# Summing layer 0's softmax denominators from probabilities that DMAs have folded from 128 keys to 64

## The chip, the cores and the metric

The kernel runs on one core of a Trainium2 chip. A core has a matrix engine (TensorE, PE in the profile, with its weight loads shown as PEld), a vector engine (VectorE, DVE), a scalar engine (ScalarE, ACT), GpSimd (POOL), a queue that mostly issues transfers (SyncE, SP) and 16 DMA engines that all queues share. Each engine works through its own instructions in order. The metric is the time of one execution on the device in microseconds (us). Three timed executions of the kernel before took 994.68, 995.34 and 997.74 us; the median, 995.34 us, is what the prediction is held against.

## The reference, cut to what matters

Two cross-attention layers follow each other over the same 128 context tokens. There are 2 batches of 2048 query tokens, width 512 and 16 heads. Only layer 0 is touched, and of it only the sum in the softmax:

```python
qh = (q @ Wq + bq)                                 # 16 heads of 64
attn = einsum('bqhd,bkhd->hbqk', qh, kh) * mask    # masked scores are 0, not -inf
attn = attn - max(attn)                            # one maximum over the whole tensor
attn = exp(attn) * mask
attn = attn / (sum(attn, axis=-1) + 1e-15)         # sum over the 128 keys
out  = einsum('hbqk,bkhd->bqhd', attn, vh) @ Wo + bo
x    = layernorm(out + residual) * gamma + beta
```

Layer 1 repeats the pattern with 16 heads of 32, an ordinary softmax and its own output projection and layer norm.

## The kernel before, in words

The 4096 query tokens are cut into 8 blocks `t` of 512. Layer 0's attention handles a block in 4 groups `g` of 4 heads, so there are 32 steps (t, g). They go in the list `order`: blocks are taken two at a time, and for each group of heads the two blocks come one after the other. Two neighbouring entries of `order` (the same heads, two blocks) form a pair; the loop over `i` handles the 16 pairs. Scores and probabilities are held with the 128 keys on the partitions and the 512 queries along the row. The denominator is therefore a sum over partitions, and TensorE does it with a block of ones as weights.

Everything is issued in program order (`manual_schedule`), so the text of the loop is the order on every engine. Iteration `i` is built like this (from i = 1 on):

- `queries_pair` makes the queries of pair `i` with seven products in Strassen's manner (1, 6, 7, 2, 5, 4, 3 in this order; each is two matmuls, listed as four, because the profile shows every fp32 matmul as two instructions). The results stand in PSUM tiles of two rings of two buffers each, `mm_tile` and `av_tile`. VectorE adds them up (`add`, lines 358 and 360). Between the products, `exponentials0` is called for the two steps of pair i-1.
- `exponentials0` (lines 420 to 434) needs the largest score of the step. VectorE reduces a row of maxima (line 427), scales it (428), ScalarE takes the exponential of two halves (431) and GpSimd multiplies each half with the mask (432).
- `scores0` for the first step of pair `i` (the matmuls of line 394), VectorE multiplies by the mask and finds the partial maxima (406), SP stores them to DRAM (415, tensor `top`) and loads all of them back onto every partition (418, tile `every`). SP waits at line 418 until the store of line 415 has landed.
- `attend0` for the first step of pair i-1: four matmuls with `ones` sum the keys (442, tile `den`), ScalarE copies the sums (444), eight matmuls make the unnormalised outputs `psu` (450), ScalarE copies them (454), and SP stores 8 KB of sums (455) and 512 KB of outputs (458).
- `scores0` for the second step of pair `i`, then `attend0` for the second step of pair i-1.

In this order a round trip ties one iteration to the next: the second step's maxima of iteration i-1 go to DRAM and back (415, 418) and end at line 427 in the middle of iteration i's products. VectorE's adds of products 5, 4 and 3 stand behind line 427 in VectorE's queue. Below, "top1" and "every1" are the store and the load for the second step, "top0" and "every0" those for the first.

A few things differ at the ends. The iterations of the first two blocks (i = 0 to 3) also make the keys. Masks of later blocks are loaded from GpSimd's queue (line 233) and blocks of `xT` from SP's (226). After the loop the last steps are finished, the sums come back from DRAM as reciprocals, and GpSimd multiplies the outputs with them (line 182) ahead of layer 0's projection (625).

## Time and profile before

The profiled execution took 995.52 us on the device; the span from its first to its last instruction is 993.4 us. It stands 0.18 us from the median of the three timed ones.

| engine | busy us | share of the span | instructions |
|---|---|---|---|
| PE | 968.4 | 97% | 4628 |
| DVE | 657.6 | 66% | 1060 |
| POOL | 482.8 | 49% | 403 |
| ACT | 382.2 | 38% | 625 |
| DMA queue of SP | 125.03 MB | 36.9% of 16 engines | 49536 packets |
| DMA queue of POOL | 2.10 MB | 0.7% of 16 engines | 1152 packets |

The groups that the change touches, over the whole run:

| line | engine and operation | count | busy us | mean ns of one |
|---|---|---|---|---|
| 442 | PE, sums with ones, 128 rows by 32 columns | 256 | 34.1 | 605 |
| 450 | PE, outputs psu, 128 by 32 | 512 | 62.6 | 598 |
| 394 | PE, scores, 64 by 128 | 256 | 63.9 | 616 |
| 432 | POOL, mask multiply | 64 | 150.1 | 2367 |
| 444 | ACT, copy of the sums | 32 | 18.8 | 589 |
| 233 | POOL, issue of a mask load, 256 KB | 8 | 4.7 | 583 |

How to read it: several small matmuls run side by side in the array, so the sum of busy time is less than count times mean. The loop of layer 0 takes the first 377 us; the rest is layer 0's projection and all of layer 1. An engine that is busy 97% may still wait here and there, so where a stage is bound is read from the chain of waits and from the timeline of each engine, not from the share. Times in the timelines are microseconds from the start of the span.

### The profile page before, as it was taken

To read this page: it belongs to the slowest core of one execution; us is meant where nothing else is said; L and a number is where in the kernel's file an instruction comes from. 1 tells how busy PE (TensorE), PEld (TensorE's weight loads), DVE (VectorE), ACT (ScalarE), POOL (GpSimd) and SP (SyncE) were. 2 spreads that over 40 slices of the span, in tenths; PEclk is the share of its full clock that TensorE was granted. 3 is DMA by queue.
4 is the path that set the end of the run, shared out by engine and by line. 5 is a ranking of instruction groups with operands and counts; after the bars stand their busy time and mean duration, and the time that the engine had idled before them with its cause. 6 is when DMAs were issued, how large, how long until landed. Compare 5 with 4: busy or idle time off the path is not lost.

```text
span 993.4 us, 12731 instructions
## 1 busy us (share of the span) xinstructions
PE 968.4 (97%) x4628; PEld 450.2 (45%) x4628; DVE 657.6 (66%) x1060; ACT 382.2 (38%) x625; POOL 482.8 (49%) x403
## 2 busy tenths in 40 slices
PE   8999999999999999999999999999999999999896
PEld 4444333333333334474544645545545545446432
DVE  2544645564465543148569879779789699698766
ACT  1133334334433344034544334444344344344251
POOL 1043544543454545695453934926736637445142
PEclk9999999999999999999999999999999999999998
DMA  9314254224223344633632532622724624304211
GB/s 341 135 49 142 56 167 154 54 76 151 69 59 98 123 139 131 197 119 136 257 123 86 222 121 85 258 85 92 274 71 141 243 84 167 124 1 175 82 43 42
DMA packets 51326, 128.46 MB, mean 129 GB/s; under 512 B 9441, under 2 KB 13281, under 8 KB 47681
## 3 DMA queue, kind: packets, MB, share of 16 engines
q1 hardware_dynamic: 49536, 125.03, 36.9%
q0 software_dynamic: 1152, 2.10, 0.7%
q8 instruction: 36, 0.59, 0.3%
q10 hardware_dynamic: 576, 0.53, 0.2%
q14 instruction: 26, 0.21, 0.1%
HBM read 101.46 MB, written 26.18 MB: 128 GB/s over the span
## 4 chain that ended last, share of the span: by engine, by line
PE 72%; DVE 12%; DMA 9%; issue 2%; POOL 2%; ACT 1%; SPq 1%; POOLq 0%; ACTq 0%; DVEq 0%
PE pso L625 18%; PE ps L346 17%; PE st L394 6%; PE pso L970 6%; PE psu L450 5%; DMA r<-rows 5%; PE psq L776 3%; PE den L442 3%; PE mx L827 3%; DVE sums L857 2%; PE s L900 2%; PE u L948 2%; DVE bn L607 2%; PE psq L814 1%; PE psq L327 1%
## 5 line engine op out<-in xcount | busy, mean ns | idle before, releaser
L432 POOL TENSOR_TENSOR sm<-sm,mask 128x1024 f32<-128x1024 f32 x64 | 150.1, 2367 | 214.0 <-ACT sm L431 214.0
L625 PE MATMUL pso<-wo,uT 128*128 128x512 f32 x512 | 229.3, 599 | 1.1 <-POOL uT L182 1.1
L625 PEld LDWEIGHTS pso<-wo,uT 128*128 128x128 f32 x512 | 94.5, 190 | 118.1 <-issue 108.0
L612 POOL TENSOR_TENSOR rstd<-rstd,mhalf 128x1 f32<-128x1 f32 x64 | 35.1, 549 | 222.0 <-DVE shift L616 221.9
L970 PE MATMUL pso<-wq,ctx 128*128 128x512 f32 x256 | 115.1, 600 | 0.0
L406 DVE CUSTOM_DVE_ANT_1 sm<-st,mask 128x1024 f32<-128x1024 f32 x64 | 75.8, 1221 | 45.2 <-issue 18.5
L431 ACT ACTIVATE sm<-sm,ncs 128x1024 f32<-128x1024 f32 x64 | 69.9, 1140 | 73.8 <-DVE ncs L428 73.6
L843 ACT ACTIVATE e<-mx,less 128x128 f32<-128x128 f32 x224 | 61.0, 383 | 83.3 <-DVE less L840 83.3
L924 ACT ACTIVATE p<-p 128x2048 f32<-128x2048 f32 x28 | 53.5, 1911 | 101.2 <-DVE p L919 70.4
L358 DVE TENSOR_TENSOR q<-ps,q 128x512 f32<-128x512 f32 x75 | 51.5, 689 | 55.1 <-PE ps L346 31.0
L919 DVE TENSOR_TENSOR p<-s,p 128x1024 f32<-128x1024 f32 x56 | 65.9, 1218 | 31.4 <-PE s L900 29.7
L346 PE MATMUL ps<-xt,wq 128*128 128x512 f32 x180 | 83.4, 599 | 0.0
L182 POOL TENSOR_TENSOR uT<-uT,r 128x1024 f32<-128x1024 f32 x32 | 75.2, 2358 | 6.6 <-PE psv L536 4.3
L970 PEld LDWEIGHTS pso<-wq,ctx 128*128 128x128 f32 x256 | 46.7, 190 | 57.6 <-issue 50.7
L857 DVE TENSOR_REDUCE sums<-e 128x16 f32<-128x2048 f32 x28 | 63.8, 2278 | 1.1 <-ACT e L851 1.1
L394 PE MATMUL st<-q,k 64*128 64x512 f32 x256 | 63.9, 616 | 0.2 <-DVE q L358 0.2
L450 PE MATMUL psu<-sm,v 128*32 128x512 f32 x512 | 62.6, 598 | 0.0
L346 PE MATMUL ps<-t,s 128*128 128x512 f32 x120 | 56.4, 592 | 0.0
L346 PEld LDWEIGHTS ps<-xt,wq 128*128 128x128 f32 x180 | 33.2, 190 | 46.5 <-issue 44.5
L444 ACT COPY dens<-den 128x512 f32<-128x512 f32 x32 | 18.8, 589 | 86.6 <-PE den L442 86.6
L640 ACT ACTIVATE z<-z,shift,rstd 128x512 f32<-128x512 f32 x32 | 26.0, 813 | 67.7 <-POOL shift L617 67.7
L642 POOL TENSOR_TENSOR y<-z,g 128x512 f32<-128x512 f32 x32 | 40.6, 1269 | 23.1 <-ACT z L640 23.1
(148 smaller groups left out, 1463.3 us busy)
## 6 DMA issues: line engine op xcount, KB each, us to landing
p<-rows SPq DMA_DIRECT2D x28, 1024.0 KB
u<-u SPq DMA_DIRECT2D x32, 512.0 KB
uT<-u SPq DMA_DIRECT2D x32, 512.0 KB
xt<-in_xT_dram SPq DMA_DIRECT2D x16, 512.0 KB
z<-in_x_dram SPq DMA_DIRECT2D x32, 256.0 KB
r<-r SPq DMA_DIRECT2D x32, 256.0 KB
out_dram<-y SPq DMA_DIRECT2D x32, 256.0 KB
r<-rows SPq DMA_DIRECT2D x28, 256.0 KB
```

What stands on the lines that cost most here:

```text
L182: nc.gpsimd.tensor_tensor(u, u, r.unsqueeze(1).to_broadcast([P, 2, TB]), ALU.mult)
L346: nc.tensor.matmul(ps, w[:, c, :], x[c] if isinstance(x, tuple) else x[:, c, :], start=(c == 0), stop=(c == 1),)
L394: nc.tensor.matmul(st[n][:, j, :], k0[rows, 2 * g + n, b * K : (b + 1) * K], q[rows, :], start=True, stop=True,)
L406: nc.vector.tensor_tensor_reduce(out=sm, in0=st[n], in1=masks[t].unsqueeze(1).to_broadcast([P, 2, TB]), scale=1.0, scalar=-3.4028234e38, o ...
L431: nc.scalar.activation(s, s, AF.Exp, bias=ncs[:, i + n : i + n + 1])
L432: nc.gpsimd.tensor_tensor(s, s, masks[t].unsqueeze(1).to_broadcast([P, 2, TB]), ALU.mult)
L450: nc.tensor.matmul(ps[32 * j : 32 * (j + 1), :], v0[:, b, d : d + 32], p[j], start=True, stop=True,)
L625: nc.tensor.matmul(ps, uTs[t, n // 2][:, n % 2, i * P : (i + 1) * P], wo0s[n // 2][:, n % 2, :], start=(n == 0), stop=(n == NE - 1),)
L843: nc.scalar.activation(e[:, r, i, :], ps[1][:, r - 2, i, :], AF.Exp, bias=less[:, r - 2, i : i + 1], scale=scaling,)
L857: nc.vector.tensor_reduce(to.rearrange("p r i o -> p r (i o)"), open_x.pop((t, g)), AX.X, ALU.add)
L919: nc.vector.tensor_tensor(p1[:, at], ps[n], p1[:, at], ALU.subtract)
L970: nc.tensor.matmul(ps, ctxs[t][g][:, i * P : (i + 1) * P], wo1s[:, g, :], start=(g == 0), stop=(g == NG - 1),)
```

## The change

For the first 14 of the 16 pairs the denominators are no longer summed in `attend0`. After the two steps of pair i-1 are masked, `fold(i-1)` issues four DMAs from GpSimd's queue. Two plain copies (512 KB each) put keys 0 to 63 of the pair's first step on partitions 0 to 63 of a tile `f`, and keys 64 to 127 of its second step on partitions 64 to 127. Two accumulating DMAs (512 KB each) then add the other 64 keys of each step to the same rows. `f` so holds both steps, each with 64 rows in place of 128. One iteration later, after `queries_pair` and before the scores, `sums_of_folded(i-2)` sums that tile with eight matmuls of 64 rows by 32 columns, alternating between the upper and the lower 64 partitions and writing to two PSUM tiles; ScalarE copies both and SP stores both.

To make room and to free the ring `av_tile` for this, three things move: product 3 of `queries_pair` takes its PSUM tile from `mm_tile`; the tiles `den` come from a pool of two buffers in place of four; and the rows `g1s`, `b1s` (layer 1's gamma and beta) are loaded after the first list of layer 1's steps, behind `wo1s`, in place of before the loop. The tile `f` has one buffer.

```diff
-            add(c12, product(3, s4[:, g], b22, av_tile), c12)
+            add(c12, product(3, s4[:, g], b22, mm_tile), c12)
...
+        FOLDED = NB // 2 * NG - 2
...
+            pairs0[t, g] = pair
...
+        def store_sums(t, g, ps):
+            den = a2.tile([P, TB], F32, tag="den", name=f"dens0_{t}_{g}")
+            nc.scalar.copy(den, ps)
+            nc.sync.dma_start(
+                den_rows(den_dram, t, g), den.rearrange("(j n) q -> j n q", n=32)[:, 0, :]
+            )
+        def fold(i):
+            f = w1.tile([P, 4, TB], F32, tag="fold", name=f"fold_{i}")
+            p = [pairs0[step].rearrange("p n j q -> p (n j) q") for step in order[2 * i : 2 * i + 2]]
+            rows = [slice(0, P // 2), slice(P // 2, P)]
+            for n in range(2):
+                nc.gpsimd.dma_start(f[rows[n]], p[n][rows[n]])
+            for n in range(2):
+                nc.gpsimd.dma_start(f[rows[n]], p[n][rows[1 - n]], accum_op=ALU.add)
+            folded[i] = f
+
+        def sums_of_folded(i):
+            f = folded.pop(i)
+            ps = [av_tile(f"den0_{i}_{n}") for n in range(2)]
+            for j in range(4):
+                for n in range(2):
+                    rows = slice(n * P // 2, (n + 1) * P // 2)
+                    nc.tensor.matmul(
+                        ps[n][32 * j : 32 * (j + 1), :], ones[rows, :], f[rows, j, :],
+                        start=True, stop=True,
+                    )
+            for n in range(2):
+                store_sums(*order[2 * i + n], ps[n])
...
         def attend0(t, g):
-            ps = av_tile(f"den0_{t}_{g}")
-            for j in range(4):
-                nc.tensor.matmul(ps[32 * j : 32 * (j + 1), :], ones, p[j], start=True, stop=True)
-            den = a4.tile([P, TB], F32, tag="den", name=f"dens0_{t}_{g}")
-            nc.scalar.copy(den, ps)
+            if order.index((t, g)) // 2 >= FOLDED:
+                ps = av_tile(f"den0_{t}_{g}")
+                for j in range(4):
+                    nc.tensor.matmul(ps[32 * j : 32 * (j + 1), :], ones, p[j], start=True, stop=True)
+                store_sums(t, g, ps)
...
-            nc.sync.dma_start(
-                den_rows(den_dram, t, g), den.rearrange("(j n) q -> j n q", n=32)[:, 0, :]
-            )
...
-        g1s, b1s = row(const, g1, "g1"), row(const, b1, "b1")
...
                 queries_pair(p, g, order[2 * i - 2 : 2 * i])
+                if i > 1:
+                    sums_of_folded(i - 2)
+                if i - 1 < FOLDED:
+                    fold(i - 1)
...
             nc.sync.dma_start(wo1s, chunks(wo1))
+            g1s, b1s = row(one, g1, "g1"), row(one, b1, "b1")
```

## The prediction

> **What bounds the kernel now.** I read the page first, then the chain of waits over the loop of layer 0, and then the timelines of PE, DVE, SP and POOL around one iteration.

> ```profile
> PE 968.4 (97%) x4628; PEld 450.2 (45%) x4628; DVE 657.6 (66%) x1060; ACT 382.2 (38%) x625; POOL 482.8 (49%) x403
> ```

> TensorE is busy 97% of the span. The chain of waits for iteration i = 12 (columns: start, length, what) shows no gap:

> ```profile
> 290.40 12.21 PE ps L346 x28
> 302.62 1.92 PE st L394 x8
> 304.54 1.00 PE den L442 x8
> 305.53 1.77 PE psu L450 x16
> 307.31 1.92 PE st L394 x8
> 309.23 0.99 PE den L442 x8
> 310.22 1.77 PE psu L450 x16
> 312.00 12.21 PE ps L346 x28
> ```

> An iteration is 21.6 us of matmuls back to back: products 12.21, twice scores 1.92, sums 1.00 and outputs 1.77. From i = 4 on, only i = 5 breaks it, for 0.2 us. So work taken off TensorE counts, unless the round trip of the maxima then becomes the longer loop. The next views show how near it is. First PE (products 4 and 3 of the same iteration), then DVE, whose bracket is its idle time before:

> ```profile
> 299.02 1.88 PE L346 MATMUL ps<-t,wq 128*128 128x512 f32 x4
> 300.74 1.88 PE L346 MATMUL ps<-xt,s 128*128 128x512 f32 x4
> ```

> ```profile
> 299.33 0.42 DVE L427 TENSOR_REDUCE whole<-every 128x2 f32<-128x256 f32 x1 [1.07 <-DMA every<-top]
> 299.79 0.17 DVE L428 TENSOR_SCALAR ncs<-whole 128x2 f32<-128x2 f32 x1
> 299.86 0.68 DVE L358 TENSOR_TENSOR q<-ps,q 128x512 f32<-128x512 f32 x1
> 300.46 0.74 DVE L360 SCALAR_TENSOR_TENSOR q<-ps,db,q 128x512 f32<-128x512 f32 x1
> 301.12 0.68 DVE L358 TENSOR_TENSOR q<-ps,q 128x512 f32<-128x512 f32 x1
> ```

> DVE stands idle until every1 lands. The two adds that read product 5 end at 301.20, which is 0.46 us after product 3 has started. Before, that is harmless: product 3 has an `av_tile`. Then SP:

> ```profile
> 289.58 0.32 SPq L415 DMA_DIRECT2D top<-top  x1
> 295.90 0.32 SPq L418 DMA_DIRECT2D every<-top  x1
> ...
> 306.22 0.33 SPq L415 DMA_DIRECT2D top<-top  x1
> 309.49 0.32 SPq L418 DMA_DIRECT2D every<-top  x1
> ...
> 310.45 0.76 SPq L458 DMA_DIRECT2D u<-u  x1
> 311.31 0.38 SPq L415 DMA_DIRECT2D top<-top  x1
> ```

> top0 lands after 3.3 us. top1 is issued right behind the 512 KB store of outputs and lands only after 6.3 us (289.58 to 295.90); every1 takes another 3.4, so T, from the issue of top1 to DVE's reduction, is 9.75 us here. In the twelve iterations i = 4 to 15 T is between 8.56 and 10.9 us, mean 9.88.

> **The change part by part.**

> *Sums on TensorE.* For 14 pairs two passes of 0.995 us go and one pass of eight smaller matmuls comes. No row has eight side by side. The `psu` row has four in 0.885 us (1.77 for two groups), the scores two. If all eight overlap, a pass is about 1.0 us and 14 x 0.99 = 13.9 us go; if only four do, it is 1.9 and 1.3 us go. I take 1.0: line 827 issues 32 matmuls with their weight loads in 1.17 us, 37 ns each, so 16 need 0.6 us to issue and issue does not bind. [...]

> *Product 3 in `mm_tile`.* The ring has two buffers and was used by 1, 6, 5, 4; now product 3 takes product 5's buffer and must wait for both adds that read it, which stand behind line 427 on DVE. This is the wait that the change adds. Behind it on PE stand product 3, the new pass, both scores and outputs; behind those stands top1, which the next line 427 waits for. That closes a loop, and its length replaces the sum over PE if it is longer. From DVE's reduction: 1.87 us to the end of the second add and 0.06 to wake PE; product 3 1.81 (300.74 to 302.55); new pass 1.00; scores 1.92 and outputs 1.77 up to the second scores; from those to top1 4.07 (307.24 to 311.31). That is 12.5 us, and with T = 9.75 the loop is 22.25 us against 21.6 now: **+0.65 us per iteration although PE has 1 us less to do**. Its low end is 21.83 (DVE's scan of the second scores ends 3.65 us after they start, and SP then issues at once), its high end 22.5 (T of 10.0). For the 12 iterations i = 4 to 15: +7.8 us, between +3 and +11.

> *The folding DMAs.* Four issues on POOL at 0.56 us, 2.2 us per iteration. POOL works 9.4 us in 21.6, and is free from 305.96 to 315.75. Per fold 1 MB is copied and 1 MB accumulated. The nearest row is a pair of mask loads, 512 KB, from the same queue:

> ```profile
> 219.26 1.12 POOL L233 DMA_DIRECT2D mask<-in_maskT_dram  x2
> ```
> ```profile
> 219.80 0.32 SPq L415 DMA_DIRECT2D top<-top  x1
> 223.77 0.32 SPq L418 DMA_DIRECT2D every<-top  x1
> ```

> The DMA engines are busy with them from 220.5 to 222.5, 262 GB/s; one lands after 3.7 us (median). By the same rate the two copies move in 4.0 us and land about 6.2 us after the first issue (1.2 to the first byte, 1.0 after the last). The accumulates wait for that, on POOL; behind them there stand the next step's masks, 9.8 us later, so this wait is covered. The accumulates move in 4.0 us, or 8.0 if reading both operands counts twice.

> What they meet is the round trip. POOL's masks of the second step end 6.63 us after line 427 (299.33 to 305.96), and top0 goes out 8.4 us after it, so the copies run beside top0. Beside the mask loads top0 took 3.97 us, and 4.39 at 132.96, against 2.8 to 3.6 otherwise: +1.0 us. SP issues nothing until top0 has landed, so the output store and top1 go out that much later. The accumulates start some 13 us after line 427, as does the 512 KB output store that top1 must follow. Alone it moves from 290 to 292.7. Shared, it ends later by some part of the accumulates' 4.0 us; I take half, +2.0. The bounds are 0 (different engines or moments) and 6. So +3.0 us on T in the 11 iterations i = 5 to 15, whose round trip runs beside a fold: **+33 us**, between 0 and +75. [...]

> *The first iterations.* At i = 1 both passes go and none comes: -2.0. At i = 2 and 3 the making of keys (3.65 us) gives the round trip room: at i = 3 line 427 runs at 103.33 without a wait, and T = 9.8 from its store would have it ready at about 101.2. The folds' 3.0 us and the 1 us gained use that up: 0, at best -1.0 each. Sum -2, between -4 and 0.

> *Moves that cost nothing by these rows.* ScalarE still copies two sums per iteration, 0.59 us each, now ahead of the outputs; it waits for PE 2.3 us and more before each today, and without that cover they would cost 1.2 us per iteration. SP's two 8 KB stores (0.50 us each) come before top0, when SP is idle, instead of before the output store; without that cover, 1.0. Two buffers for `den` in place of four: the store of 8 KB has a whole iteration to land; without it, one landing, 3 us. The loads of `g1s` and `b1s` leave SP's queue at 23 us and come at 443 us, ahead of residual loads: 512 KB, at most 2.0 us, and layer 1's first use is at 553 us. The residual loads are the cover, so 0 to +2.

> **Sum.** +7.8 + 33 - 2 = +38.8 us on the profiled execution's 995.5, which is 0.2 above the median: 1034 us.

> **The rivals.**

> *The transfers hide (nothing lost to contention).* DMA engines are 37% busy, and the store and the accumulates could miss each other. Against: both wait for transfers that land within a us of each other. It leaves +7.8 - 4 = +4: **999 us**, between 994 and 1002.

> *It becomes faster.* The one thing that decides is T. PE alone would need 20.6 us, so with 12.5 us of work in the loop, T below 8.1 us frees all of it, and below 9.1 us breaks even. That could happen because SP no longer has the 8 KB store between every0 and the output store, so that store leaves earlier. Price: the full -13.9, **981 us**. Against: T was below 9.1 only once in twelve.

> *The fold comes late.* PE needs it 3.74 us after the next line 427, so it has 22.25 + 3.74 - 6.63 = 19.4 us. Copies 6.2, two issues 1.1, accumulates 8.0 + 2.2: 17.5, in time. At a quarter of the copy rate (16 us) it is 25.5, and PE waits 6 us each time: 12 x 6 + 4 = **+76, 1071 us** or more.

> *The eight matmuls run four at a time.* The pass then saves nothing and lies in the loop: 14 x 0.9 = 12.6 more, **1047 us**. Against: issue is quick enough, and each half has its own PSUM tile.

> **How the numbers follow.** Forecast 0.59 (its own range 1010 to 1072), hidden 0.17, faster 0.10, late 0.09, four at a time 0.05. A measurement of this kernel can tell about 0.3%, 3 us. Of the hidden case a third lies within 3 us of no change and hardly any below: faster 0.11, same 0.06, slower 0.83. The range runs from 996, which leaves out the faster case and the low end of the hidden one, to 1078, which leaves out the slowest half of the late fold.

> **What would show it.** In the profile after, product 3 should start about 1.9 us after line 427 and not right behind product 4, with PE idle before it (some 4 us per iteration), DVE's idle time at 427 grown by as much, and an iteration of about 25 us. SP should show top1 landing after more than 8 us and top0 after more than 4. The new pass should take 1.0 us. If PE waits at the new pass instead, the fold was late; if iterations are 20.6 us, T has shrunk and I am wrong. [...]

## The result and the profile after

The changed kernel takes 1115.23 us (median of four executions, 1112.64 to 1116.18) where the kernel before, on the same chip, takes 995.54. The ratio is 1.119 (95% interval 1.117 to 1.122). The direction and the mechanism were as forecast; the size was not: +120 us came where +38.8 was forecast, and the time lies above the range. The profiled execution took 1115.53 us, its span is 1113.7 us. Nearly all of the loss is in the loop of layer 0: product 3 of the last iteration starts at 479.85 us in place of 365.51, which is 114.3 us later.

First the page of the kernel after (engines; clock in 40 slices; the queue of GpSimd's transfers with packets, MB and share of 16 engines; the two groups that say most, with busy time, mean of one and idle time before; the fold's transfers with median us to landing):

```profile
PE 997.2 (90%) x4628; PEld 454.4 (41%) x4628; DVE 657.5 (59%) x1060; ACT 381.5 (34%) x625; POOL 520.8 (47%) x459
PEclk9998997898888988889999999999999999999998
q0 software_dynamic: 5632, 31.46, 14.7%
L346 PE MATMUL ps<-xt,s 128*128 128x512 f32 x60 | 52.3, 1022 | 72.4 <-DVE q L360 72.4
L455 POOL DMA_DIRECT2D fold<-sm x28 | 23.3, 834 | 82.4 <-DMA fold<-sm 82.4
fold<-sm POOLq DMA_DIRECT2D x56, 512.0 KB, 6.7
```

TensorE is no longer busy all the time. It stands 72.4 us ahead of product 3 (the group `ps<-xt,s`) and waits there for line 360, the second of the two adds that the prediction named. In 8 iterations it also waits ahead of product 4, 17.2 us in all, for an add (line 358) behind the first step's reduction; the prediction had no such wait, but product 3 still starts only when the second round trip is over. And it got slower: it has 14 passes less to do, yet its busy time rose from 968.4 to 997.2 us, and its granted clock, 0.997 in the mean before, is 0.951, with 8s and a 7 in the slices of the loop.

The chain of waits over one iteration (start, length, what; the small "issue" steps between are left out):

```profile
312.69 9.12 DMA top<-top
...
321.83 3.87 DMA every<-top
...
325.72 0.43 DVE whole L429
...
326.35 0.59 DVE q L358
326.94 0.67 DVE q L360
...
327.65 3.78 PE ps L346 x4
331.44 1.50 PE den L464 x16
332.93 1.92 PE st L395 x8
334.85 0.51 PE psu L485
335.36 1.14 DVE sm L408
...
336.54 5.60 DMA top<-top
...
342.62 0.41 SPq L490
...
343.08 8.85 DMA top<-top
```

In the kernel before this chain was matmuls only. Now it is the loop of the prediction, from top1 (312.69) round to the next top1 (343.08): 30.4 us, of which three transfers take 18.6 us. Product 3 starts 1.93 us after line 429 (the reduction that had line 427 before), to the hundredth as forecast. Against the forecast four things stand out: product 3 takes 3.78 us in place of 1.81, top0 lands after 5.60 us, top1 after 9.12 and 8.85, and top1 goes out only behind top0's landing and the store (line 490) on SP, 2.3 and 2.8 us after VectorE's scan has ended.

The timeline of PE around it (bracket: idle before, and what ended it):

```profile
318.88 1.88 PE L346 MATMUL ps<-t,wq 128*128 128x512 f32 x4
327.65 3.78 PE L346 MATMUL ps<-xt,s 128*128 128x512 f32 x4 [6.89 <-DVE q L360]
331.37 1.57 PE L464 MATMUL den<-fold,ones 64*32 64x512 f32 x16
```

Product 4 takes 1.88 us; product 3, the same four instructions after a gap of 6.89 us, takes twice that. The windows of the same kernel show why (window; length; busy time and count of PE, PEld, DVE, ACT, POOL; then the granted clock, DMA share and GB/s):

```profile
324.00:325.00 1.00, 0.00 (x0) 0.00 (x0) 0.00 (x0) 0.00 (x0) 0.00 (x0) 1.00 1.05 216
325.00:326.00 1.00, 0.00 (x0) 0.00 (x0) 0.28 (x1) 0.00 (x0) 0.00 (x0) 0.80 0.79 324
...
331.00:332.00 1.00, 1.00 (x9) 0.23 (x16) 0.53 (x1) 0.00 (x0) 1.00 (x1) 0.50 0.00 0
332.00:333.00 1.00, 1.00 (x18) 0.14 (x4) 0.17 (x1) 0.00 (x0) 0.31 (x1) 0.79 0.00 0
```

The clock falls from full to one half in the gap (the mean of the window from 325 is 0.80), stays there through all of product 3 and most of the new pass, and comes back in the window from 332.

Last, the issues of the fold on GpSimd, one iteration earlier by its data:

```profile
303.41 1.11 POOL L453 DMA_DIRECT2D fold<-sm  x2 [0.82 <-POOL sm L434]
308.07 0.85 POOL L455 DMA_DIRECT2D fold<-sm  x1 [3.56 <-DMA fold<-sm]
311.06 0.81 POOL L455 DMA_DIRECT2D fold<-sm  x1 [2.14 <-DMA fold<-sm]
```

The copies go out at 303.4 and top0 at 306.3. The accumulates go out at 308.1 and 311.1, the 512 KB store of outputs at 311.9 and top1 at 312.69, so the second accumulate, the store and top1 fall within two microseconds. In windows of one and two microseconds from 305 to 318 us the DMA engines' busy share is 0.86 or more throughout.

**Where the 120 us are.** From the starts of product 3 in the two traces: at i = 2, 3 and 4 the kernel after is 4.5, 10.9 and 17.8 us behind, at i = 15 114.3. So some 18 us are lost up to i = 4 and 8.78 us in each of the 11 iterations after, 30.42 in place of 21.64 us. The loop and its forecast, as means over those 11:

| part of the loop | forecast us | measured us |
|---|---|---|
| reduction to the start of product 3 | 1.93 | 2.09 |
| product 3 | 1.81 | 3.53 |
| new pass | 1.00 | 1.56 |
| from the pass to the issue of top1 | 7.76 + 1.0 | 10.31 |
| T, top1 to the reduction | 9.75 + 2.0 | 12.92 |
| sum | 25.25 | 30.41 |

From the reduction to product 3 it is 1.93 us in eight of the iterations and 2.17 to 2.72 us in i = 7, 11 and 12, where the scaling of line 430 takes 0.41 to 0.96 us in place of 0.17. GpSimd's mask multiply runs beside it there; in the 26 cases of this trace without one, line 430 takes 0.17 us. The means of product 3, the pass and the part up to top1 go by i = 4 to 14, those of T and of the reduction by i = 5 to 15, as the loop runs.

### The profile page after: what moved, and what is told of

Read it like the earlier page. It is cut to its first block, busy times and chain, and to the rows that moved or that the text cites. A ratio compares the mean times of both kernels' runs of the same rounds, so it can differ in the third digit from the quotient of the medians.

```text
span 1113.7 us, 12852 instructions
## 1 busy us (share of the span) xinstructions
PE 997.2 (90%) x4628; PEld 454.4 (41%) x4628; DVE 657.5 (59%) x1060; ACT 381.5 (34%) x625; POOL 520.8 (47%) x459
## 3 DMA queue, kind: packets, MB, share of 16 engines
q0 software_dynamic: 5632, 31.46, 14.7%
## 4 chain that ended last, share of the span: by engine, by line
PE 47%; DMA 29%; DVE 16%; issue 3%; POOL 2%; SPq 2%; ACT 1%; POOLq 0%; ACTq 0%; DVEq 0%
DMA top<-top 17%; PE pso L660 14%; PE ps L346 6%; PE pso L1005 5%; DMA r<-rows 5%; DMA every<-top 4%; PE st L395 4%; PE psq L811 3%; PE mx L862 2%; PE den L464 2%; DVE sums L892 2%; DVE sm L408 2%; PE psu L485 2%; PE u L983 2%; PE s L935 2%
## 5 line engine op out<-in xcount | busy, mean ns | idle before, releaser
L346 PE MATMUL ps<-xt,s 128*128 128x512 f32 x60 | 52.3, 1022 | 72.4 <-DVE q L360 72.4
L429 DVE TENSOR_REDUCE whole<-every 128x2 f32<-128x256 f32 x30 | 12.6, 419 | 168.2 <-DMA every<-top 168.2
L346 PE MATMUL ps<-xt,wq 128*128 128x512 f32 x180 | 83.4, 599 | 0.0
L358 DVE TENSOR_TENSOR q<-ps,q 128x512 f32<-128x512 f32 x75 | 51.6, 687 | 50.8 <-PE ps L346 47.3
L455 POOL DMA_DIRECT2D fold<-sm x28 | 23.3, 834 | 82.4 <-DMA fold<-sm 82.4
L489 ACT COPY u<-psu 128x512 f32<-128x512 f32 x64 | 37.5, 586 | 70.2 <-PE psu L485 70.2
L346 PEld LDWEIGHTS ps<-xt,s 128*128 128x128 f32 x60 | 16.2, 297 | 100.7 <-DVE q L360 86.6
```

The costliest lines, as they stand in the source:

```text
L346: nc.tensor.matmul(ps, w[:, c, :], x[c] if isinstance(x, tuple) else x[:, c, :], start=(c == 0), stop=(c == 1),)
```

## The experiments

Each time is the median of 2 to 10 executions, each ratio is to the kernel before on the same chip. "The changed kernel" is the one above.

### Product 3 back in its old ring

```diff
-            add(c12, product(3, s4[:, g], b22, mm_tile), c12)
+            add(c12, product(3, s4[:, g], b22, av_tile), c12)
```

> The changed kernel with one part undone: product 3 takes its PSUM tile from av_tile again, as before; the folds, their DMAs and the late pass of sums stay. Theory A (the wait of product 3 on the adds behind line 429 closes the loop): product 3 and the pass of sums leave the loop, and the next thing that waits for VectorE's adds is the second pair of score matmuls, 2.5 us after the reduction of line 429. Loop: 2.5 + 0.96 + 1.85 to the second scores, some 5.9 from there to top1, round trip 13 us: about 24 us in place of 30.4, so about 75 us less over 13 iterations, 1030 to 1055 us. TensorE's idle time moves to line 395 and shrinks to some 3 us. Theory B (the contention is what costs, wherever the wait stands): the round trip of 13 us is unchanged and PE waits as long at the scores, 1095 to 1115 us.

Measured: 1096.73 us, ratio 1.102 (1.100 to 1.104). Product 3 indeed no longer waits, and yet only 18 us come back. The timeline of PE for this kernel says where the wait went:

```profile
310.66 1.04 PE L464 MATMUL den<-fold,ones 64*32 64x512 f32 x2
318.90 1.96 PE L464 MATMUL den<-fold,ones 64*32 64x512 f32 x14 [7.20 <-DVE q L358]
```

The `av_tile` ring has two buffers and serves products 7, 2 and 3 and now two tiles `den` in a row. The second `den` takes the buffer of product 3 and waits for its add, which stands behind the reduction on VectorE all the same: 56.2 us in 14 waits, up to 7.2. This miss is a step that was overlooked in the expectation and not a refutation of the loop: the new pass with its two tiles is held up behind the same queue whichever ring product 3 uses. So the loop doesn't need the move of product 3 to `mm_tile`; the early pass alone suffices.

### The move of product 3 alone, in the kernel before

```diff
-            add(c12, product(3, s4[:, g], b22, av_tile), c12)
+            add(c12, product(3, s4[:, g], b22, mm_tile), c12)
```

> The kernel before with one part of the change alone: product 3 takes its PSUM tile from mm_tile; no folds, sums as before. Theory A: the loop of the prediction without contention, 22.25 us against 21.6 for the iterations from i = 4 on, +3 to +11 us, so 998 to 1007 us, with a wait of product 3 of about half a microsecond to 1 us in each iteration. Theory B (without the fold's transfers this wait is nothing): 994 to 997 us.

Measured: 1001.16 us, ratio 1.006 (1.005 to 1.008), that is +5.9 us, where the prediction's term for it was +7.8 (3 to 11). An iteration takes 22.08 us (mean from i = 4 to 15) where the formula gave 22.25; with this run's own T, 9.60 us in the mean, it gives 22.10. The gaps before product 3 are at most 1.2 us and its matmuls stay at full clock (1.98 us). The wait is what the prediction said it is, where it stands without the transfers.

### The changed kernel without its transfers

```diff
-            f = w1.tile([P, 4, TB], F32, tag="fold", name=f"fold_{i}")
-            ... four transfers from GpSimd ...
-            folded[i] = f
+            folded[i] = f_once        # written once, with ones
```

> The changed kernel without the four DMAs of each fold: the tile that the pass of sums reads is written once with ones, so the denominators are wrong and only the transfers are left out; the pass, the wait of product 3 and the order stay. Theory A with contention as the source of the long round trip: the loop falls to its value without contention, 22.25 us, and 992 to 1003 us come out; TensorE's clock stays at 1.0 because its gaps are under 1.5 us. Theory C (the transfers do not matter, the order on the queues alone lengthens the loop): above 1060 us.

Measured: 1020.69 us, ratio 1.026 (1.023 to 1.028): 25 us over the kernel before, where the expectation (992 to 1003) had next to nothing. So the transfers, with all that they set off, account for 1115 - 1020 = 95 of the 120 us, and the loop alone for the other 25. PE in one of its iterations:

```profile
294.89 3.53 PE L346 MATMUL ps<-xt,s 128*128 128x512 f32 x4 [2.40 <-DVE q L360]
298.35 1.09 PE L459 MATMUL den<-f_once,ones 64*32 64x512 f32 x16
```

An iteration takes 23.85 us here where the formula of the prediction gives 22.25. By the same table: from product 3 to the scores 3.49 in place of 2.81 (half clock in four of the iterations, where product 3 takes 3.22 to 3.53 us), T 10.57 in place of 9.75, the rest within 0.1. So a part of T's growth is there without any transfer of a fold: top1 lands after 7.3 us in the mean, 6.3 in the kernel before. The early iterations, on the other hand, went as forecast: product 3 of i = 3 starts at 103.57, 2.3 us earlier than in the kernel before (105.89). So the 18 us lost there in the changed kernel belong to the transfers.

### TensorE kept busy ahead of product 3

```diff
+            filler = av_tile(f"filler_{p}_{g}")
+            for _ in range(6):
+                nc.tensor.matmul(filler, ident, b22[:, 0, :], start=True, stop=True)
             add(c12, product(3, s4[:, g], b22, mm_tile), c12)
```

> The changed kernel with six extra fp32 matmuls of 128x128 by 512 (5.2 us, their result unused) between products 4 and 3, where TensorE stands idle for 4.7 to 7.6 us. Theory D (the halved clock after the gap adds to the loop): product 3 takes 1.8 us in place of 3.78 and the pass of sums 1.0 in place of 1.0 to 1.96, 2.4 us per iteration for 13 iterations, about 30 us less, 1078 to 1092 us, although TensorE has 78 us more to do. If the slow product 3 is not from the idle time: no gain, 1110 to 1135 us.

Measured: 1106.29 us, ratio 1.112 (1.109 to 1.115): 9 us back, not the 23 and more that were expected.

```profile
316.23 3.58 PE L346 MATMUL ps<-t,wq 128*128 128x512 f32 x4 [2.36 <-DVE q L358]
319.60 5.45 PE L382 MATMUL filler<-xt,ident 128*128 128x512 f32 x12
324.89 1.88 PE L346 MATMUL ps<-xt,s 128*128 128x512 f32 x4
326.70 1.09 PE L467 MATMUL den<-fold,ones 64*32 64x512 f32 x16
```

With the gap filled, product 3 takes 1.88 us again and the new pass 1.09; over the run, product 3 is busy 33.4 us in place of 52.3 and the pass 16.7 in place of 22.9. That the clock, and not the tile or the operand, made them slow is thus shown. But product 4 still has a gap ahead of it in some iterations (7 waits, 15.6 us) and takes 3.58 us in the one shown, in place of 1.88, and the filler itself ends after the add is ready. The clock was worth some 25 us of work; a gap that is merely filled gives little of it back.

### The second step's exponentials behind all adds

```diff
-            exponentials0(*before[1])        # ahead of product 4 and 3, and of the adds of 5
...
             add(c12, product(3, s4[:, g], b22, mm_tile), c12)
+            exponentials0(*before[1])
```

> The changed kernel with one reordering: the exponentials of the second step (line 429 on VectorE and what follows) are issued after the seven products' adds instead of between them. Folds and their DMAs are as in the change. In the run with product 3 in av_tile the wait only moved to the pass of sums, which there needed product 3's add; here no product, add or pass stands behind the reduction of line 429. Theory A (the loop is closed by that queueing on VectorE): the round trip of 13 us only has to meet the second step's outputs, 6.63 us after line 429; two iterations may then share one round trip plus 19 us of PE work, 22 to 23 us per iteration in place of 30.4, so 995 to 1020 us. Theory B (the transfers cost this time wherever PE waits): 1085 to 1115 us.

Measured: 1040.18 us, ratio 1.045 (1.041 to 1.048): **75 us back**, from a change of order alone: two instructions of VectorE (lines 429 and 430), with the exponentials and masks that follow them, now stand behind the adds. Neither expected range was met: the lower one (995 to 1020) was too low, the upper one (1085 to 1115) is refuted. With that reduction last, none of the adds for products 5, 4 and 3 stands behind the second round trip, PE has no gap before product 3, and the loop of the prediction is open. Not all of the 75 us need be due to that: the later masks also put the fold at another moment, and top1 lands after 7.8 us in the mean in place of 9.3. What is left, from the waits of PE (total, times, longest):

```profile
PE psu L485 <- ACT dens L440: 15.1, 10, 6.3
PE den L464 <- DMA fold<-sm: 13.9, 9, 3.8
```

The fold now comes late, since the second step's probabilities are masked later: with the waits of single weight loads in it, the pass takes 2.96 us in the mean of the 14, against 1.02 where it waits for nothing. And the outputs wait for ScalarE's copies of the sums, which stand behind the late exponentials.

### The first step's output store behind the second round trip

```diff
-                attend0(*order[2 * i - 2])
+                attend0(*order[2 * i - 2], hold=True)     # its 512 KB store isn't issued yet
...
             scores0(*steps0[1])
+            store_u()                                     # after the load of every1
```

> The changed kernel with one reordering on SP: the 512 KB output store of the first step is issued after every1 instead of ahead of top1. Theory A: top1 no longer follows 512 KB on the same queue beside the accumulates; its landing falls from 9.1 us to 4 to 6, the loop by 3 to 5 us, and the gap of PE falls to 2 to 4 us: 1045 to 1080 us. If the accumulates alone hold up top1: above 1100 us.

Measured: 1084.72 us, ratio 1.089 (1.084 to 1.094), short of the expected 1045 to 1080. SP's queue in this kernel:

```profile
295.42 0.62 SPq L417 DMA_DIRECT2D top<-top  x1
304.63 0.32 SPq L420 DMA_DIRECT2D every<-top  x1
```

Now top1 goes out directly behind every0 and without a large store ahead of it. It lands after 9.2 us here, which is the longest of the 11 iterations; the mean is 7.6 us against 9.3 in the changed kernel. T falls from 12.92 to 11.29 us in the mean. So the store accounts for some 1.6 us of T. The same order of stores without the fold's transfers (`no_fold_u_behind`, below) has a T of 8.88 us, so that beside the fold another 2.4 us remain with no large store ahead of top1.

### Copies in place of the accumulating transfers

```diff
-                nc.gpsimd.dma_start(f[rows[n]], p[n][rows[1 - n]], accum_op=ALU.add)
+                nc.gpsimd.dma_start(f[rows[n]], p[n][rows[1 - n]])
```

> The changed kernel with the two accumulating DMAs of a fold replaced by plain copies of the same rows and bytes, behind the same waits; the addition is left out, so the denominators are wrong. Theory E (adding costs the DMA engines more than copying): the second pair of transfers gets shorter, from 7.2 us to landing to 5 or less, the round trip by 1 to 2 us, and the time falls by 15 to 40 us to 1075 to 1100. Theory F (the bytes alone matter): 1110 to 1120 us.

Measured: 1088.51 us, ratio 1.093 (1.090 to 1.097), in the expected range (1075 to 1100) of the reading that accumulating costs more than its bytes. From the page of this kernel:

```profile
q0 software_dynamic: 5632, 31.46, 13.0%
L455 POOL DMA_DIRECT2D fold<-sm x28 | 14.3, 512 | 88.0 <-DMA fold<-sm 88.0
fold<-sm POOLq DMA_DIRECT2D x56, 512.0 KB, 5.1
```

The same bytes in the same places: the accumulates take GpSimd 834 ns to issue and a plain copy 512; the second pair lands after 7.2 us (median) as accumulates and 5.0 as copies; T is 12.92 and 11.35 us. 27 of the 95 us are therefore due to the accumulation and 68 would be there with plain copies.

### Both moves together, and their controls

`both_moves` is the changed kernel with the two edits above (late exponentials, store behind). `no_fold_both_moves` is the same without the transfers, `before_both_moves` is the kernel before with the two edits, and `before_u_behind` and `no_fold_u_behind` have the store's move alone.

> The changed kernel with both reorderings: second step's exponentials behind the adds, first step's output store behind every1. Theory A: the round trip is short enough and nothing of PE's queue stands behind it, so PE is the bound again with 20.6 us per iteration: 980 to 990 us, below the kernel before, if the fold lands in time (it needs 15 us from the first issue, the pass comes about 15.7 us after). If folds are late, PE waits at the pass: 990 to 1010 us.

> The run without the folds' DMAs (tile of ones, wrong denominators) with both reorderings. Theory A: what is left is the pass of sums alone, PE is the bound with 20.6 us per iteration and the full saving of the prediction's first term shows: 995.5 - 13.9 = 981.6, so 979 to 986 us. If something else than the transfers and the queueing behind line 429 also costs (the copies of sums on ScalarE, the smaller matmuls): 988 to 1000 us.

> The kernel before with both reorderings and nothing else, as the control: PE is the bound there, with 21.6 us per iteration and no wait to take away, so 993 to 997 us by theory A. If the reorderings help by themselves: below 992 us.

> The run without the folds' DMAs (tile of ones, wrong denominators) with the first step's output store behind every1 and the second step's exponentials where the change has them. In the run with both reorderings and without DMAs the outputs waited 1.2 us in each iteration for ScalarE's copies of the sums, which stood behind the late exponentials; here they do not. Theory A: without the 512 KB ahead of it top1 lands after some 4 us and every1 after 4 more, T about 8 us, below the 8.1 of the prediction's faster rival; PE is the bound with 20.6 us per iteration: 980 to 988 us, so the first term's 13.9 us are real. If the pass saves nothing: 994 us or more.

> The kernel before with the first step's output store behind every1 alone, the control of the other run: PE is the bound with 21.6 us per iteration, no wait is on the path, 993 to 998 us.

| kernel | us | ratio (95%) |
|---|---|---|
| both_moves | 1021.21 | 1.029 (1.023 to 1.034) |
| no_fold_both_moves | 1003.35 | 1.008 (1.006 to 1.010) |
| before_both_moves | 1006.77 | 1.011 (1.008 to 1.013) |
| no_fold_u_behind | 995.79 | 1.000 (0.999 to 1.002) |
| before_u_behind | 994.92 | 1.000 (0.998 to 1.001) |

The first three missed in the same direction, and the control shows a reason that they share: in the kernel before, where nothing else was changed, the two moves cost 11 us, and the store's move alone costs nothing (`before_u_behind`). The waits of PE in `no_fold_both_moves`:

```profile
PE psu L482 <- ACT dens L440: 16.2, 14, 1.2
```

ScalarE copies the sums (line 440) only after the second step's two exponentials, which now come just then; the outputs `psu` need the PSUM buffers that those copies free, and PE waits up to 1.2 us in each of 14 iterations. So the move that frees VectorE's queue ties up ScalarE's. In `before_both_moves` these waits are shorter (4.3 us in 15), and the second step's sums, whose weight loads now wait for GpSimd's masks, take 1.4 us or more in place of 1.06. In `both_moves` the fold comes late as well: its pass takes 2.09 us in the mean.

`no_fold_u_behind` missed too (980 to 988 was expected), and in an instructive way. Part of its chain:

```profile
266.13 4.53 DMA top<-top
...
270.67 4.49 DMA every<-top
...
275.18 0.43 DVE whole L429
...
277.24 1.98 PE ps L346 x4
279.22 1.02 PE den L459 x16
```

T is 9.05 us here and 8.88 in the mean. The prediction had said that below 9.1 the change breaks even and that it needs 8.1 for the full gain; by its formula 8.88 would make 21.4 us. The iteration takes 21.70 us against 21.64, since product 3 starts 2.22 us after the reduction in the mean in place of 1.93 (line 430 runs beside a mask here, too: 0.71 us at 297.00 in place of 0.17), and the kernel takes what it took before. The formula holds within 0.3 us, and without its transfers the fold's whole saving on TensorE is still eaten by this loop.

### The second step's exponentials between the adds

The middle way: `exponentials0(*before[1])` behind the two adds that read product 5, ahead of those of products 4 and 3, so that product 3's buffer comes free before the round trip ends; and the store behind, as above. Once without the transfers, once with them.

```diff
-            exponentials0(*before[1])
             add(c22, ps, c21)
             add(c12, ps, c12, less1)
+            exponentials0(*before[1])
```

> The run without the folds' DMAs (tile of ones, wrong denominators), output store behind every1, and the second step's exponentials between: behind the two adds that read product 5 and ahead of the adds of products 4 and 3. Product 3 then no longer waits for every1, and ScalarE's exponentials end some 13 us into the iteration, about when its copies of the sums are wanted. Theory A: PE is the bound at last, 20.6 us per iteration, 980 to 986 us: the saving of 13.9 us is there and the round trip was what hid it. If the pass really saves less than 1 us per iteration: 990 us or more.

> The changed kernel, folds and all, with the same two reorderings as the run beside it. Theory A: with the folds' transfers the round trip is 12 to 13 us, every1 comes 12 to 13 us into the iteration, after product 3 and about when the first scores need it; PE then waits some 1 to 2 us per iteration for exponentials, masks or the fold's landing: 995 to 1020 us, and faster than the kernel before only if nearly all of the round trip is covered.

Measured without transfers: 984.31 us, ratio 0.988 (0.986 to 0.990). PE has no gap in the loop, and the pass of eight matmuls starts at

```profile
230.71 1.09 PE L459 MATMUL den<-f_once,ones 64*32 64x512 f32 x16
...
251.49 1.09 PE L459 MATMUL den<-f_once,ones 64*32 64x512 f32 x16
...
272.26 1.09 PE L459 MATMUL den<-f_once,ones 64*32 64x512 f32 x16
```

that is every 20.8 us, where the prediction had put PE's own work at 20.6. The saving on TensorE is real: 11.4 of the 13.9 us that the prediction counted.

Measured with the transfers: 1005.89 us, ratio 1.011 (1.006 to 1.015). With the same fold this is 109 us faster than the changed kernel; it is still slower than the kernel before. From the waits of PE, in an execution of 1012.22 us:

```profile
PE psu L487 <- ACT dens L440: 6.8, 10, 1.1
PE ps L346 <- DVE q L358: 3.4, 1, 3.4
PE den L464 <- DMA fold<-sm: 1.6, 2, 0.9
PEld den L464 <- DMA fold<-sm: 8.9, 11, 1.8
```

The difference to the run without transfers, 21.6 us between the medians and 24.5 between the two profiled executions, is what the fold costs here. Most of it is the fold's late landing. The last line is of the weight loads: one matmul of the pass runs, the others wait for the second half of the fold, and PE counts as busy meanwhile. The 14 passes take 24.6 us up to the scores where they take 14.3 without the transfers. These 10.3 us and the waits of `psu` and `ps` make 20.5 of the 24.5.

### The addition on VectorE

Two plain copies per pair bring only the missing 64 keys to their partitions, and VectorE adds its own 64 keys one iteration later; with both moves.

```diff
-                nc.gpsimd.dma_start(f[rows[n]], p[n][rows[n]])
-            for n in range(2):
-                nc.gpsimd.dma_start(f[rows[n]], p[n][rows[1 - n]], accum_op=ALU.add)
+                nc.gpsimd.dma_start(f[rows[n]], p[n][rows[1 - n]])
+        def add_folded(i):
+            for rows, p in parts:
+                nc.vector.tensor_tensor(f[rows], f[rows], p[rows], ALU.add)
```

> The changed kernel with both reorderings, and a fold that moves half the bytes: two plain copies of 512 KB bring the other 64 keys of each step into the tile, and two VectorE additions of 64 rows by 2048 add the own 64 keys one iteration later, behind the first step's reduction. Theory A: the transfers of a fold fall from some 11 us of all DMA engines to about 5, POOL no longer waits for landings, and the loop lies between the 20.6 us of PE alone and the 22.6 us of the run with both reorderings: 985 to 1010 us. If the fold's cost is not in its bytes: 1015 to 1025 us as with both reorderings.

Measured: 1086.74 us, ratio 1.091 (1.088 to 1.094), far from the expected 985 to 1010.

```profile
300.22 6.64 DVE L461 TENSOR_TENSOR fold<-fold,sm 64x2048 f32<-64x2048 f32 x2
```

Two adds of 64x2048 take 6.64 us, right behind the first reduction and ahead of the products' adds, so product 4 waits for VectorE (50.9 us in 14 waits). The first of them takes 2.28 us and the second, which runs beside GpSimd's masks, 4.3. This trades the transfers for a queue in the same place. The transfers' share did fall as meant, from 14.7 to 6.7% of 16 engines.

## Why the prediction was right about the sign and wrong about the size

**Right.** The wait is where the prediction put it and is released by what it named: product 3 starts 1.93 us after the reduction. Taken alone it costs 5.9 us (7.8 forecast). The formula "12.5 us plus T" holds within 0.3 us in two runs that were made later: with their own T it gives 22.10 us for `p3_mm_alone` (22.08 measured) and 21.4 for `no_fold_u_behind` (21.70). The new pass of eight matmuls takes 1.0 us at full clock, as taken, and the four-at-a-time rival is out. The fold isn't late in the changed kernel: neither PE nor its weight loads wait for `fold<-sm` anywhere. The rival "the transfers hide" is out, by 95 us.

**Wrong, by the terms of the sum.** The forecast's 38.8 us and the 114.3 us measured up to the last product 3 differ by 75.5. Steps 1 to 3 below make up 74, and the way from the reduction to product 3 (2.09 in place of 1.93) the other 2.

1. *"So +3.0 us on T in the 11 iterations ... +33 us."* The mechanism was right and the value too low. By the table the pass-to-top1 part is 10.31 us in place of 7.76 without contention, and T 12.92 in place of 9.75: +5.7 us per iteration in place of +3.0, 63 us in all, 30 more than forecast. That is inside the step's own bounds (0 to 75). By `no_fold_dma` 0.9 of the 5.7 us are there without a transfer (T 10.57, the other part 7.86), which the 9.75 read from the kernel before leaves out. The fold's own share is then 4.8 us, and two sizes in it were off. The copies were costed at 262 GB/s, the rate of the mask loads from DRAM. The fold in fact occupies all 16 engines for 11.2 us: 14.7% of 1113.7 us is 163.7, less 7.0 for the mask loads (0.7% of 993.4), over 14 folds; that is 2 MB at 187 GB/s, where 8.0 us was taken. And accumulates cost more than copies of the same bytes (`plain_copies`: 7.2 us to landing against 5.0). One transfer of the fold lands after 5.9 us (median) as a copy and 7.2 as an accumulate in the changed kernel, both beside other transfers. That the fold, issued from GpSimd, holds up what SP issues shows in T: with no large store ahead of top1 it is 11.29 us beside the fold and 8.88 without.
2. *The clock.* The sum has no term for it, and no row of the kernel before showed one: the granted clock there is 0.997 in the mean. Product 3 and the pass together take 5.09 us in place of 2.81, +2.28 in each of the 11 iterations: 25 us. `pe_kept_busy` shows that this is the clock. The prediction had forecast gaps of 4 us itself; such a row could not be in a trace whose PE hardly stands still in the loop (0.2 us from i = 4 on).
3. *"The first iterations ... Sum -2, between -4 and 0."* With 0.65 of the next term for i = 4, this was a forecast of -1.3 against +17.8 measured: 19 us. Without transfers product 3 of i = 3 does come 2.3 us early, so the -2 was right for everything but the fold. The room that the prediction saw (2.1 us between the forecast 101.2 and line 427 at 103.33; by its own rows, top1 at 91.04 and T = 9.8, it is 100.8 and 2.5 us) was less than what the transfers took: T at i = 3 is 14.3 us (top1 out at 100.59, reduction at about 114.9), not 9.8 plus 3.0.
4. *Moves at nothing.* They held in the changed kernel: no wait of PE in the loop names ScalarE's copies of sums. The price given for a lost cover there, up to 1.2 us per iteration, is what `no_fold_both_moves` paid when its reordering took the cover away (up to 1.22 us in each of 14).

Steps 1 and 2 are not independent. A longer T makes a longer gap, after the gap the clock is lower (0.50 behind the one of 6.89 us), and the slow product 3 stands in the same loop. That the loop is what turns them into time is shown by `exps_late`: with all transfers still there, moving the reduction behind the adds takes 75 of the 120 us away, though some of it may be due to the transfers' other moment.

What stays open: the last 4 us between product 3 of the last iteration (+114.3) and the end of the loop (+118.5), why top1 lands a microsecond later in `no_fold_dma` than in the kernel before, and how the 2.4 us that T keeps beside the fold divide between copies and accumulates.

## What to carry to other kernels

When a change shortens the engine that bounds a loop, look for the queue in which its releases stand behind a round trip: once that loop is the longer one, whatever new transfers add to the trip is paid in every iteration, and where the release stands in the queue may be worth more than the change (75 us here by one new order, 109 by another with the store moved too, against 11 that the fold could save). A forecast gap on TensorE needs its clock in the sum (25 us here), even where the trace of before shows none. And a control on the kernel before is worth its run: without it the 11 us that the reordering itself cost would have been put down to the fold.
